# Copying the diagonal quarter of one rearrangement with ScalarE in the Gram stages

## The chip, the cores and the metric

The kernel runs on one core of one Trainium2 chip. The metric is the device time of one execution in microseconds (us). Engines are named by their work: TensorE (PE, with its weight loads PEld), VectorE (DVE), ScalarE (ACT), GpSimd (POOL) and SyncE (SP, which here only issues transfers).

## The reference, cut to what matters

Two bottleneck blocks of a ResNet follow each other on x of shape (64, 1024, 14, 14), all in float32. Each block normalises over the whole batch, so every normalisation needs statistics of all 12544 pixels (64 images of 196):

```python
def _bn(x, gamma, beta):
    mean = jnp.mean(x, axis=(0, 2, 3), keepdims=True)
    var = jnp.var(x, axis=(0, 2, 3), keepdims=True)
    xn = (x - mean) * jax.lax.rsqrt(var + EPS)
    return gamma.reshape(1, -1, 1, 1) * xn + beta.reshape(1, -1, 1, 1)

out = jax.nn.relu(_bn(_conv(x, w1, b1, 1, 0), g1, be1))      # 1x1, 1024 -> 256
out = jax.nn.relu(_bn(_conv(out, w2, b2, 1, 1), g2, be2))    # 3x3, 256 -> 256
out = _bn(_conv(out, w3, b3, 1, 0), g3, be3)                 # 1x1, 256 -> 1024
out = jax.nn.softplus(residual_scale)[0] * out
return jax.nn.relu(x + out)
```

## The kernel before

The 256 channels between the convolutions lie in `y_all`, as 128 partitions by two slots by 12544 pixels, and stay on the chip. In time the program is: the first 1x1 convolution of block 0; then for each block its 3x3 convolution (`conv2`), its Gram stage (`gram` and `conv3_stats`) and its last convolution. The last convolution of block 0 is fused with the first of block 1 (`fused`), that of block 1 stands alone (`final`).

The Gram stage is where the change is. The last normalisation needs mean and variance of 1024 channels that are a linear map of 256. The kernel doesn't compute the 1024 channels for that. It takes the 256x256 matrix of products of the 256 channels over all pixels (a Gram matrix), together with the sums of the channels, and derives the statistics from it in `conv3_stats`. TensorE sums over partitions, so for the Gram matrix the pixels have to lie on the partitions: `y_all` has to be transposed, 128 pixels of 256 channels at a time. The unit of work is a chunk of 256 pixels (`px`), 49 chunks in a stage. For each chunk eight matmul calls on a tile `zt` follow, four for each 128 pixels (half a chunk); there are six `zt` tiles (`NZT`) in rotation.

The transpose is made in one of two ways:

- `by_tensor` (line 1081): TensorE transposes into a PSUM bank, VectorE adds `c_row` and writes `zt`. Eight chunks go this way, the pieces in `still`.
- `by_vector` (line 1099): VectorE transposes blocks of 32x32 (line 1102), one instruction for each chunk. Such a transpose swaps partitions and pixels only inside groups of 32 partitions, so the data must first be moved between the four groups of 32 partitions. For this, `move(k)` (line 1058) copies piece `moved[k]` of `y_all` with transfers into a tile, its home: group j of the partitions, quarter i of the piece's pixels, to group i, column block j. There are 4x4 such pairs (i, j). Where i equals j the data keeps its partitions.

`moved` has seven pieces: `moved[0]` with 1280 pixels (five chunks) and `moved[1]` to `moved[6]` with 1536 (six chunks). For `moved[0]` and `moved[1]` all sixteen pairs are transfers. From `moved[2]` on, `move(k)` leaves out the four pairs with i equal to j and `stay(k)` (line 1051) copies them with four ScalarE activations, each on 32 partitions by 768 elements. The homes take turns, `homes[k % 3]`; in block 0 `homes[1]` is the tile `ws`, which is why the transfers of `moved[1]` and `moved[4]` have `ws` in the profile there and `home` in block 1.

Each transfer is issued on SyncE's queue or on GpSimd's. A line in `move` settles which, from the transfer's number n, and `keep_in_program_order` fixes the order of the issues. Before a piece can be moved, ScalarE applies the normalisation and relu (`normed`, two activations for a piece) and VectorE subtracts a constant for each channel (`less`, line 1041, one instruction for each slot).

The order of all this is written out by hand in the generator `pairs` (line 1109). It yields one `zt` after the other, and after certain chunks it emits the work for pieces to come. In the part with `by_tensor`, n is the number of the chunk: after chunk 3 the norms of `moved[1]`, after 4 its `less`, `move(1)` and the norms of `moved[2]`, after 5 and 6 the two halves of `less` of `moved[2]`, after 6 the norms of `moved[3]`, after 7 `move(2)` and `stay(2)`. In the part with `by_vector`, piece k emits `less` of piece k + 2 after its chunks 1 and 3, then `move(k + 2)`, the norms of `moved[k + 3]` and `stay(k + 2)`. Matmuls, activations through the helper `act`, the transposes and the issues hold the written order on their engine; what isn't held in this way is placed by the framework's planner.

Every `by_vector` chunk of a piece needs the whole piece in its home: all its transfers and, where there is one, its `stay`.

Of the kernel before, what the change touches and what calls it, by code (L numbers as in the profile page):

```python
# [88 lines left out]
def bottlenecks(ctx: ExitStack, tc: tile.TileContext, x, w1s, w2s, w3s, pars, out):  # L89
    nc = tc.nc  # L90
# [82 lines left out]
    def busy(psum, tag, n, with_=None):  # L173

        v = ident if with_ is None else with_
        for i in range(n):
            matmul(psum.tile(448, tag), v, v[:, :1].to_broadcast([P, 448]), start=True, stop=True)
# [154 lines left out]
    def act(*args, **kw):  # L332

        tc.keep_in_program_order(nc.scalar.activation(*args, **kw))  # L334

    class Conv1(Seven):
# [15 lines left out]
        def sum(self, i):  # L352
            return self.pool.tile([P, CS // 2, self.n], FP, tag=f"at{i}", name=f"at{i}")
# [195 lines left out]
    def norm_vector(s, y, aff):  # L549

        scale, shift = aff
        tc.keep_in_program_order(
            nc.vector.tensor_scalar(y, y, scale[:, s : s + 1], shift[:, s : s + 1], ALU.mult, ALU.add)
        )
        tc.keep_in_program_order(nc.vector.tensor_scalar(y, y, 0.0, None, ALU.max))
# [441 lines left out]
    def gram(psum, pool, homes, aff, minus_c, beside):  # L997
# [39 lines left out]
        def normed(a, e, slots=both):  # L1037
            for s in slots:
                norm(s, y_all[:, s, a:e], aff, act)

        def less(a, e, slots=both):
            for s in slots:
                y = y_all[:, s, a:e]
                tc.keep_in_program_order(nc.vector.tensor_scalar(y, y, minus_c[:, s : s + 1], None, ALU.add))

        def home(k):
            a, e = moved[k]
            x = homes[k % 3][:, : MS * (e - a)].rearrange("p (s j f) -> p s j f", s=MS, j=4)
            return x, a, (e - a) // 4

        def stay(k):

            x, a, run = home(k)
            for i in range(4):
                here = slice(32 * i, 32 * i + 32)
                act(x[here, :, i], y_all[here, :, a + i * run : a + i * run + run], AF.Copy)

        def move(k):
            x, a, run = home(k)
            for i, j in itertools.product(range(4), range(4)):  # L1060
                if k > 1 and i == j:
                    continue
                n = 4 * i + j if k < 2 else 3 * i + j - (j > i)
                queue = nc.gpsimd if (n % 2 if k < 2 else n in (1, 3, 6, 8, 10)) else nc.sync
                ins = queue.dma_start(
                    out=x[32 * i : 32 * i + 32, :, j], in_=y_all[32 * j : 32 * j + 32, :, a + i * run : a + i * run + run]
                )
                tc.keep_in_program_order(ins)
# [3 lines left out]
        def center_row():  # L1072

            ps = psum.tile(M, "ax")
            for s in range(MS):
                matmul(
                    ps[:, s * P : (s + 1) * P], minus_c[:, s : s + 1].to_broadcast([P, P]), ident, start=True, stop=True
                )
            act(c_row, ps, AF.Copy)

        def by_tensor(a):
            tp = psum.tile(CH * M)
            for c in range(CH):
                for s in range(MS):
                    tc.keep_in_program_order(
                        nc.tensor.transpose(
                            tp[:, (c * MS + s) * P : (c * MS + s + 1) * P],
                            y_all[:, s, a + c * P : a + (c + 1) * P], ident,
                        )
                    )  # L1090
            zt = next(zts)
            tc.keep_in_program_order(
                nc.vector.tensor_add(
                    zt[:, :, 1 : M + 1], tp.rearrange("p (c m) -> p c m", c=CH), c_row[:, None, :].to_broadcast([P, CH, M])
                )
            )
            return zt

        def by_vector(k, i):
            zt, x = next(zts), home(k)[0].rearrange("p s j f -> p (s j) f")  # L1100
            tc.keep_in_program_order(
                nc.vector.transpose(
                    zt[:, :, 1 : M + 1].rearrange("p b (n c) -> p b n c", c=32),
                    x[:, :, i * CH * 32 : (i + 1) * CH * 32].rearrange("p n (b r) -> p b n r", r=32),
                )
            )
            return zt

        def pairs():

            for a in 0, px:
                norm_vector(1, y_all[:, 1, a : a + px], aff)
                normed(a, a + px, (0,))
            normed(2 * px, 4 * px, (0,))
            center_row()
            rest = [(piece, s) for piece in still for s in range(MS)]
            (second, end), half = still[1], sum(still[1]) // 2
            for n, a in enumerate(a for piece in still for a in range(*piece, px)):
                yield by_tensor(a)
                if n == 0:  # L1120
                    busy(psum, "ax", 1)
                    norm_vector(1, y_all[:, 1, 2 * px : 4 * px], aff)
                    normed(*moved[0])
                elif n == 1:
                    less(*moved[0])
                    move(0)
                    normed(second, end, (0,))
                    normed(second, half, (1,))
                elif n == 3:
                    norm_vector(1, y_all[:, 1, half:end], aff)  # L1130
                    normed(*moved[1])
                elif n == 4:
                    less(*moved[1])
                    move(1)
                    normed(*moved[2])
                elif n == 5:
                    less(*moved[2], both[:1])
                elif n == 6:
                    less(*moved[2], both[1:])
                    normed(*moved[3])  # L1140
                elif n == 7:
                    move(2)
                    stay(2)
            for k, (a, e) in enumerate(moved):
                for i in range((e - a) // px):
                    yield by_vector(k, i)
                    if i in (1, 3) and k and k + 2 < len(moved):
                        less(*moved[k + 2], both[i // 2 : i // 2 + 1])
                        if i == 3:
                            move(k + 2)  # L1150
                            if k + 3 < len(moved):
                                normed(*moved[k + 3])
                            stay(k + 2)
                    elif i in (0, 5) and k > 1 and rest:
                        piece, s = rest.pop(0)
                        less(*piece, (s,))
            assert not rest
# [3 lines left out]
        for k, zt in enumerate(itertools.chain(pairs(), (None,))):  # L1161
            if before is not None:
                for c in range(CH):
                    first, last = k == 1 and c == 0, k == total and c == CH - 1
                    v = before[:, c]
                    for q, with_ in enumerate((v[:, : 3 * Q + 1], v[:, Q + 1 :], v[:, 2 * Q + 1 :], ends(v))):
                        here = slice(q % 2 * Q, q % 2 * Q + Q)
                        to = (upper, lower)[q // 2][here]
                        to = to[:, : 2 * Q + 1] if q == 2 else to
                        if q == 3:  # L1170
                            to = to.rearrange("p (k m) -> p k m", k=2)
                        matmul(
                            to, v[:, 1 + q * Q : 1 + q * Q + Q], with_, start=first, stop=last,
                            tile_position=(0, q % 2 * Q), skip_group_check=True,
                        )
            before = zt
            if k in beside:
                beside[k]()
# [392 lines left out]
```

## Time and profile before

| what | us |
|---|---|
| median of three runs | 1929.36 |
| lowest and highest of them | 1928.34, 1930.65 |
| the profiled execution | 1929.22 |
| its span, first to last instruction | 1927.4 |

The stretches of the span, from the windows of the trace (busy us of an engine in the stretch):

| stretch, us | TensorE | VectorE | ScalarE | GpSimd | DMA share |
|---|---|---|---|---|---|
| up to 587 (first convolution and 3x3 of block 0) | 581.8 of 586 | 487.7 | 271.0 | 68.7 | 0.71, then 0.29 |
| 587 to 651, Gram stage of block 0 | 62.2 of 64 | 53.4 | 41.3 | 24.6 | 0.78 |
| 680 to 1140, fused | 460.0 of 460 | 324.6 | 252.2 | 176.7 | 0.44 |
| 1165 to 1541, end of fused and 3x3 of block 1 | 370.3 of 376 | 336.2 | 245.1 | 73.0 | 0.63 |
| 1541 to 1609, Gram stage of block 1 | 65.6 of 68 | 53.3 | 42.5 | 25.9 | 0.75 |
| 1640 to 1927, final | 282.2 of 287 | 232.6 | 190.6 | 178.3 | 0.90 |

The DMA share is the mean busy share of the core's sixteen DMA engines. In the groups of the trace, line 334 is the helper `act`, so all held ScalarE work stands under it, and line 171 is the helper of the matmuls; such groups are told apart by the names of their tiles. Line 1065 holds the transfers of `move`, 87 issues on SyncE with a median of 596 ns and 69 on GpSimd with a median of 542 ns under the name `home`. "DMA to landing" is the time from an issue until the transfer is done.

### The profile page before, as it was taken

How to read it: one execution, taken by the hardware profiler on the slowest of the kernel's cores; microseconds unless marked ns; L12 is line 12 of the kernel's file. 1: busy time of each engine (PE TensorE's matmuls, PEld its weight loads, DVE VectorE, ACT ScalarE, POOL GpSimd, SP SyncE). 2: the span in 40 equal slices, each digit the busy share in tenths (PEclk: the TensorE clock that was granted, in tenths of full speed). 3: DMA queues.
4: the chain of work that ended last, by engine and by line, in shares of the span. 5: the costliest groups of instructions: out<-in, count | busy, mean ns of one | idle time of the engine just before them, and what ended most of it. 6: DMA issues, size and time to landing. Idle time of an engine off the chain costs nothing.

```text
span 1927.4 us, 28744 instructions
## 1 busy us (share of the span) xinstructions
PE 1905.4 (99%) x10240; PEld 1600.4 (83%) x10240; DVE 1547.5 (80%) x2491; ACT 1077.5 (56%) x2140; POOL 568.5 (29%) x684
## 2 busy tenths in 40 slices
PE   9999999999999999999999999999999999999998
PEld 5555557999997799999999999989999987555554
DVE  5778767999998867677766767689999986888886
ACT  2222214677777255555555555456777682666665
POOL 0111100211204133333434334302121041666664
PEclk9999999999999999999999999999999999999999
DMA  7777634787946534444444444258788466889998
GB/s 291 273 248 273 224 143 150 201 220 211 218 164 179 194 157 168 168 171 185 180 168 168 171 181 179 106 183 210 216 205 225 129 178 236 293 325 341 329 340 297
DMA packets 198911, 409.56 MB, mean 212 GB/s; under 512 B 37168, under 2 KB 175312, under 8 KB 182256
## 3 DMA queue, kind: packets, MB, share of 16 engines
q1 hardware_dynamic: 159808, 322.04, 48.8%
q0 software_dynamic: 33344, 34.62, 8.8%
q10 hardware_dynamic: 5616, 51.06, 6.3%
q8 instruction: 81, 1.33, 0.3%
q14 instruction: 62, 0.51, 0.1%
HBM read 263.75 MB, written 115.34 MB: 197 GB/s over the span
## 4 chain that ended last, share of the span: by engine, by line
PE 92%; DVE 4%; DMA 2%; issue 1%; ACT 1%; POOL 0%; SPq 0%; DVEq 0%; ACTq 0%; POOLq 0%
PE ay L171 17%; PE cy L171 17%; PE columns L171 13%; PE cp L171 11%; PE ap L171 10%; PE m L171 7%; PE l L171 6%; PE cx L171 5%; PE ax L171 4%; PE ps L171 1%; DMA home<-y 1%; DMA x<-mid 0%; DMA out<-x 0%; DMA x<-in_x 0%; DVE v L631 0%
## 5 line engine op out<-in xcount | busy, mean ns | idle before, releaser
L334 ACT ACTIVATE cu<-cy,scale 128x196 f32<-128x196 f32 (+1 forms) x552 | 256.3, 473 | 279.2 <-PE cy L171 273.8
L171 PE MATMUL columns<-v,ub 128*128 128x224 f32 (+1 forms) x1536 | 300.8, 337 | 0.0
L334 ACT ACTIVATE x<-x,shift 128x392 f32<-128x392 f32 x452 | 255.0, 613 | 72.6 <-POOL x L493 53.5
L171 PEld LDWEIGHTS columns<-v,ub 128*128 128x128 f32 x1536 | 269.4, 189 | 2.7
L467 DVE SCALAR_TENSOR_TENSOR x<-cp,scale,x 128x196 f32<-128x196 f32 (+1 forms) x368 | 178.0, 484 | 98.7 <-PE cp L171 96.5
L171 PE MATMUL cy<-ct,ws 128*128 128x196 f32 (+1 forms) x736 | 221.9, 383 | 1.2 <-ACT cu L334 1.2
L488 POOL TENSOR_TENSOR x<-x,cu 128x196 f32<-128x196 f32 (+1 forms) x184 | 160.1, 870 | 171.9 <-ACT cu L334 163.7
L171 PE MATMUL ay<-at,ws 128*128 128x196 f32 (+1 forms) x752 | 209.2, 381 | 0.0
L493 POOL TENSOR_TENSOR x<-x,cu 128x392 f32<-128x392 f32 x124 | 126.0, 1016 | 191.3 <-DVE x L467 191.3
L171 PEld LDWEIGHTS ay<-at,ws 128*128 128x128 f32 x752 | 136.6, 190 | 33.3
L171 PEld LDWEIGHTS cy<-ct,ws 128*128 128x128 f32 x736 | 133.6, 190 | 36.3 <-ACT cu L334 4.0
L171 PE MATMUL l<-diffs,ub 128*128 128x224 f32 (+1 forms) x768 | 149.2, 337 | 2.6 <-PE columns L171 2.6
L514 POOL TENSOR_TENSOR x<-x,cu 128x392 f32<-128x392 f32 x120 | 121.9, 1017 | 86.6 <-DVE x L467 62.2
L171 PE MATMUL m<-sums,ua 128*128 128x224 f32 (+1 forms) x752 | 145.9, 337 | 1.5 <-DVE sums L625 1.5
L334 ACT ACTIVATE au<-ay 128x196 f32<-128x196 f32 (+1 forms) x141 | 53.7, 381 | 158.0 <-PE ay L171 155.2
L171 PEld LDWEIGHTS l<-diffs,ub 128*128 128x128 f32 x768 | 134.3, 189 | 4.5 <-PE columns L171 3.9
L467 DVE SCALAR_TENSOR_TENSOR x<-cx,scale,x 128x196 f32<-128x196 f32 (+1 forms) x184 | 89.1, 484 | 56.7 <-PE cx L171 56.7
L171 PEld LDWEIGHTS m<-sums,ua 128*128 128x128 f32 x752 | 131.3, 189 | 3.2 <-DVE sums L625 2.9
L171 PE MATMUL cy<-y,w 128*128 128x196 f32 (+1 forms) x408 | 125.3, 393 | 0.0
L171 PE MATMUL cx<-y,w 128*128 128x196 f32 (+1 forms) x400 | 122.7, 392 | 0.0
L171 PE MATMUL cp<-y,ws 128*128 128x196 f32 (+1 forms) x368 | 113.7, 391 | 0.7 <-DVE x L467 0.7
L875 POOL DMA_DIRECT2D y<-f x24 | 30.8, 1521 | 275.1 <-DVE f L801 246.8
(221 smaller groups left out, 4003.3 us busy)
## 6 DMA issues: line engine op xcount, KB each, us to landing
x<-in_x SPq DMA_DIRECT2D x62, 1568.0 KB, 6.7
ub<-u SPq DMA_DIRECT2D x94, 768.0 KB, 5.6
x<-mid SPq DMA_DIRECT2D x32, 1568.0 KB, 8.1
mid<-x ACTq DMA_DIRECT2D x31, 1568.0 KB, 5.1
out<-x SPq DMA_DIRECT2D x123, 392.0 KB, 5.7
ua<-u SPq DMA_DIRECT2D x94, 256.0 KB, 3.2
u<-y POOLq DMA_DIRECT2D x48, 256.0 KB, 5.6
home<-y SPq DMA_DIRECT2D x71, 96.0 KB, 3.7
```

The costliest lines, as they stand in the source:

```text
L171: tc.keep_in_program_order(nc.tensor.matmul(*args, **kw))
L334: tc.keep_in_program_order(nc.scalar.activation(*args, **kw))
L467: nc.vector.scalar_tensor_tensor(v, bank, self.scale[:, o : o + 1], v, ALU.mult, ALU.add)
L488: nc.gpsimd.tensor_add(self.part(1, 1), self.part(1, 1), u3)
L493: nc.gpsimd.tensor_add(v, v, self.u12)
L514: nc.gpsimd.tensor_add(v, v, self.u12[:, i * self.n : (i + 1) * self.n])
L875: nc.gpsimd.dma_start(out=out_rows[3][:, o], in_=fa[:, o, :full], accum_op=ALU.add)
```

## The change

`move(1)` leaves out the four pairs with i equal to j, as `move` does from `moved[2]` on, so it issues twelve transfers in place of sixteen. Their numbers n and with them their queues are those of the later pieces: seven on SyncE and five on GpSimd in place of eight and eight. `stay(1)` is called after chunk 5 of the `by_tensor` part, between the two halves of `less` of `moved[2]`; on ScalarE its four copies stand after the norms of `moved[2]` and before those of `moved[3]`. This holds for both blocks.

```diff
         def move(k):
             x, a, run = home(k)
             for i, j in itertools.product(range(4), range(4)):
-                if k > 1 and i == j:
+                if k > 0 and i == j:
                     continue
-                n = 4 * i + j if k < 2 else 3 * i + j - (j > i)
-                queue = nc.gpsimd if (n % 2 if k < 2 else n in (1, 3, 6, 8, 10)) else nc.sync
+                n = 4 * i + j if k == 0 else 3 * i + j - (j > i)
+                queue = nc.gpsimd if (n % 2 if k == 0 else n in (1, 3, 6, 8, 10)) else nc.sync
                 ins = queue.dma_start(
...
                 elif n == 5:
                     less(*moved[2], both[:1])
+                    stay(1)
                 elif n == 6:
                     less(*moved[2], both[1:])
                     normed(*moved[3])
```

## The prediction

> **What bounds the kernel now.** I read the page's first part and the chain's shares first, to see whose time counts at all.
>
> ```profile
> PE 1905.4 (99%) x10240; PEld 1600.4 (83%) x10240; DVE 1547.5 (80%) x2491; ACT 1077.5 (56%) x2140; POOL 568.5 (29%) x684
> ...
> PE 92%; DVE 4%; DMA 2%; issue 1%; ACT 1%; POOL 0%; SPq 0%; DVEq 0%; ACTq 0%; POOLq 0%
> ```
>
> TensorE is busy 99% of the span and is 92% of the chain that ended last. So a change off TensorE earns only what it takes out of TensorE's few gaps. The edit touches the two Gram stages, 587 to 650 us (block 0) and 1544 to 1608 us (block 1). There I asked for the waits of each stage, then for TensorE's rows around them. Block 0, TensorE in order of time (start, us, what):
>
> ```profile
> 608.70 0.40 PE L171 MATMUL ap<-zt 128*64 128x129 f32 x4
> 610.39 0.55 PE L171 MATMUL cp<-zt 128*64 128x193 f32 x4 [1.29 <-DVE zt L1102]
> ```
>
> Block 1, the same view, and then the windows of that stretch (length; busy and count of PE, PEld, DVE, ACT, POOL; granted clock; DMA share; GB/s):
>
> ```profile
> 1567.16 0.55 PE L171 MATMUL cp<-zt 128*64 128x193 f32 x4 [2.20 <-DVE zt L1102]
> ...
> 1568.33 0.86 PE L171 MATMUL cp<-zt 128*64 128x193 f32 x4
> ...
> 1571.55 0.58 PE L171 MATMUL cp<-zt 128*64 128x193 f32 x4
> ...
> 1572.72 0.50 PE L171 MATMUL cp<-zt 128*64 128x193 f32 x4
> ```
>
> ```profile
> 1566.00:1568.00 2.00, 0.84 (x12) 0.78 (x14) 1.60 (x3) 0.00 (x0) 0.00 (x0) 1.00 0.93 215
> 1568.00:1570.00 2.00, 2.00 (x20) 1.72 (x18) 2.00 (x4) 0.00 (x0) 0.00 (x0) 0.57 0.03 8
> 1570.00:1572.00 2.00, 2.00 (x20) 1.79 (x18) 2.00 (x4) 1.22 (x2) 0.96 (x2) 0.58 0.06 11
> ```
>
> The reader is to see three costs: TensorE stands 1.29 us in block 0 and 2.20 us in block 1 for the first transpose of `moved[1]`, and after the longer gap the clock drops to 0.57, so that half a chunk's matmuls take 1.07 us (1568.33 to 1569.40) where 0.55 is the pace elsewhere. What the transpose waits for stands in the waits of block 1:
>
> ```profile
> DVE zt L1102 <- DMA home<-y: 5.4, 1, 5.4
> ```
>
> In block 0 this wait is 3.9 us. It ends with the last of the sixteen transfers of `move(1)`. I asked line 1065 one transfer at a time. In block 0 (home is `ws`) the seventh on SP is issued at 601.7, the eighth on GpSimd at 603.0; their answers:
>
> ```profile
> L1065 SPq DMA_DIRECT2D ws<-y x1: 749/749/749, 601.7 to 601.7; - x1
> ...
> DMA to landing us min/median/max: 5.8/5.8/5.8
> ```
>
> ```profile
> L1065 POOL DMA_DIRECT2D ws<-y x1: 539/539/539, 603.0 to 603.0; - x1
> ...
> DMA to landing us min/median/max: 6.0/6.0/6.0
> ```
>
> In block 1 the seventh on SP goes out at 1558.2 and lands 4.4 us later, the eighth on GpSimd at 1559.6 and lands 5.8 us later. Last landing before: 603.0 + 6.0 = 609.0 and 1559.6 + 5.8 = 1565.4; VectorE starts at 609.63 and 1566.40, that is 0.6 and 1.0 us after.
>
> [...] the windows 597 to 609 us have a DMA share of 0.99 to 1.07 at 217 to 233 GB/s with SP and GpSimd both issuing, so fewer transfers should land sooner. [...] (0.57 for some 3.3 us after 2.20 us idle; no drop after 1.29 us)[...] the trace has 842 ns for just this copy. [...] the copies of `stay(2)` at 826 to 846 ns beside a full DMA agree.
>
> **The change, part by part.**
>
> *Removed:* four of sixteen transfers of 96 KB in `move(1)` of each stage. SP issues seven in place of eight, GpSimd five. The two queues issue in order, so the first seven slots of SP and the first five of GpSimd keep their times (600 and 540 ns an issue, GpSimd's first and third 1339 and 1004 beside `less`) and have the same bytes ahead of them; what follows, now `move(2)` one to three slots earlier, is as large as what was there. So the traced landings of these slots are the new ones: block 0, SP 601.7 + 5.8 = 607.5, GpSimd 601.4 + 5.3 = 606.7; last 607.5, 1.5 us sooner. Block 1, SP 1558.2 + 4.4 = 1562.6, GpSimd 1558.0 + 3.9 = 1561.9; last 1562.6, 2.8 us sooner. A check by bytes: four times 98,304 bytes at 217 GB/s is 1.8 us of the engines. The traced slots are taken; the lower end, 0.4 and 0.6 us, is worked out with the second rival.
>
> *What TensorE gets.* VectorE would start at 607.5 + 0.6 = 608.1, and its tile is ready 0.76 us after (609.63 to 610.39): 608.9. TensorE ends its last chunk at 609.10. The gap is gone, with 0.2 us to spare: 1.29 us gained. Block 1: 1562.6 + 1.0 + 0.76 = 1564.4 against the end of TensorE's chunk at 1564.97: gap gone, 2.20 us gained.
>
> *The half clock* goes with its gap. From 1567.16 to 1572.72 seven half chunks take 5.56 us; at 0.548 each (604.54, 605.09, 605.63 in block 0) they take 3.84. 1.72 us. [...] I take 1.72: the profiled run has it, and its 1929.22 us lie 0.14 from the median of the runs shown, the fastest of which is only 0.9 us below.
>
> *Added:* four copies of 32x768, 4 x 0.842 = 3.4 us, on ScalarE between the norms of `moved[2]` and `moved[3]`. Beside what they run:
>
> ```profile
> 587.97 13.99 ACT L334 ACTIVATE y<-y,shift,scale 128x1280 f32<-128x1280 f32 x10
> 601.86 3.41 ACT L334 ACTIVATE home<-y 32x768 f32<-32x768 f32 x4
> 605.30 3.23 ACT L334 ACTIVATE y<-y,shift,scale 128x1536 f32<-128x1536 f32 x2
> 613.98 3.44 ACT L334 ACTIVATE home<-y 32x768 f32<-32x768 f32 x4 [5.46 <-DVE y L1044]
> ```
>
> The last two of the ten are the norms of `moved[3]`, 3.23 us, so the copies start at 598.6. They need `less` of `moved[1]`, done at 597.7 (595.80 + 1.94); no wait, and they end at 602.0, 5.5 us ahead of the last transfer. Block 1: start 1555.2, `less` done at 1554.3, end 1558.6. Behind them all moves by 3.4: norms of `moved[3]` done at 605.3, needed by `less` at 609.3 (608.1 and two transposes); `stay(2)` done at 608.7, needed at 613.5; norms of `moved[4]` done at 612.0, `stay(3)` may start at 612.4 (its `less` done). The 5.46 us of idle time takes the 3.4 up. Cost nothing; without that cover, up to 3.4 us a stage.
>
> *What is late next.* The first transpose of `moved[2]`: VectorE comes at 608.1 + 5.45 (six transposes, two `less`: 609.63 to 615.08) = 613.5. SP's queue is one slot shorter, so its last is at the former 22nd place, 606.7 + 6.0 + 0.6 = 613.3. TensorE needs the tile at 609.10 + 6 x 1.096 = 615.7, so 1.5 us are left. The first of `moved[3]`: its transfers go out after `less`, 4.3 us after VectorE's start, and were used 8.4 us later (613.95 to 622.39): 620.8, tile 621.6, wanted at 622.3: 0.7 left. Block 1 by the same sums: 1563.6 + 4.3, then 8.0 (1570.7 to 1577.7, and 1.0) gives 1575.9, tile 1576.7, wanted at 1578.1. No new gap; from there TensorE sets the end of the stage. Loads and stores behind it hang on the same tiles and move with it: in the windows after 1680 TensorE is busy 40.00 of 40 up to 1880 but for 0.16 us, though DMA has 0.91 to 0.97.
>
> *Sum:* 1.29 + 2.20 + 1.72 = 5.2 us off the profiled execution's 1929.22 (its span of 1927.4 and 1.8 around it): 1924.0; on the median of 1929.36, 1924.2.
>
> **The rivals.**
>
> *Gaps close, the clock does not count* (25%). The half clock is missing in most timed runs, or a little of block 0's spare 0.2 us is lost. [...] Against: the spread of the runs is too small to show runs without it. 3.5 us, 1925.9.
>
> *The transfers land little sooner* (13%). `move(2)` now enters GpSimd's ring three slots earlier and shares the engines with SP's last transfers. For: the DMA share is full. Against: the bytes per slot are the same. If it comes down to GpSimd's eighth alone, the landings are those of SP's eighth, 602.5 + 6.1 = 608.6 and 1558.8 + 6.0 = 1564.8: 0.4 and 0.6 us sooner, the clock as before: 1928.4.
>
> *Slower* (10%): the order of what is not held changes elsewhere. Only instructions given to `keep_in_program_order` keep their place; many of the second 3x3 stage (ScalarE's copies there, VectorE's sums and most of its steps) are placed by the planner, for which this stage's ScalarE now looks busier and SP and GpSimd emptier. The place is conv2 of block 1, 48 units from 1262 to 1541 us, where TensorE has no slack. For: from 645 to 1545 us TensorE already has 6.9 us of short waits, 2.3 of them on VectorE's `sums`. Against: the stages before and after hold their order by data, and matmuls are all held. At 0.25 us more for each unit it costs 48 x 0.25 = 12 us: 1936. It undoes the gain from 5.2 / 48 = 0.11 us a unit, and shows as slower from (5.2 + 3.9) / 48 = 0.19.
>
> **How the numbers follow.** Likeliest, gaps and half clock gone: 52%, 1924.2, own range 1923.0 to 1925.4. Range 1922.8 to 1929.5: the first three cases, without the slow one. A measurement here tells no change from one of about 0.2%, 3.9 us, so faster is under 1925.5: 48 of the first case's 52 and 3 of the second: 51%; same 39%; slower 10%.
>
> **What would show it.** Twelve issues of `move(1)`, four more ScalarE copies in each stage from 598.6 and 1555.2 without a wait; VectorE's waits at its first transpose of `moved[1]` 2.4 us in place of 3.9 and about 2.6 in place of 5.4; no TensorE gap over 0.3 us there and a clock of 1.00 in that stretch; the stage shorter by 1.3 and 3.9. Wrong if a gap of like size appears at `moved[2]` or `moved[3]`, if `less` of `moved[3]` waits for ScalarE, if conv2 of block 1 changes its length, or if the time saved is lost again where the final stage waits for loads.

## The result and the profile after

| | median us | lowest to highest | runs |
|---|---|---|---|
| before | 1929.37 | 1928.27 to 1930.65 | 9 |
| after | 1923.67 | 1923.15 to 1925.45 | 9 |

The ratio is 0.9972, 95% interval [0.9962, 0.9982]: 5.7 us less on the medians, where 5.2 was forecast. The profiled executions say the same: 1929.22 before, 1923.40 after (spans 1927.4 and 1921.6).

The first part of the page and the chain's shares, after:

```profile
PE 1903.4 (99%) x10240; PEld 1597.4 (83%) x10240; DVE 1546.8 (80%) x2491; ACT 1083.9 (56%) x2148; POOL 565.1 (29%) x678
...
PE 92%; DVE 3%; DMA 1%; issue 1%; POOL 1%; ACT 1%; SPq 0%; DVEq 0%; ACTq 0%; POOLq 0%
```

ScalarE has eight activations more (2148 for 2140), which are the four copies of each stage, and 6.4 us more of work. The chain is still TensorE's. Its shares are whole per cents, 19 us each, and too coarse for a change of 5.7 us.

To see where the 5.8 us between the two profiled executions came from, I cut both traces at events that both have: the first transpose on TensorE of each stage, and the first matmul of the convolution behind it.

| stretch | before, us | after, us | difference |
|---|---|---|---|
| up to the stage of block 0 | 587.44 | 588.22 | +0.78 |
| Gram stage of block 0 | 62.97 | 60.83 | -2.14 |
| between the two stages | 893.58 | 893.04 | -0.54 |
| Gram stage of block 1 | 64.49 | 61.34 | -3.15 |
| from there to the end | 318.92 | 318.17 | -0.75 |

5.3 of the 5.8 us lie in the two stages. The 0.5 us outside can't be told from scatter: the kernels of the experiments below have the same code there, but for one with another filler at its start, and in the profiles of the others the first stretch is 587.6 to 588.4 us long and the last 317.9 to 319.0. Now the places that the prediction had shown. TensorE in block 0, after:

```profile
608.90 0.49 PE L171 MATMUL cp<-zt 128*64 128x193 f32 x4
...
609.45 0.49 PE L171 MATMUL cp<-zt 128*64 128x193 f32 x4
```

Here there is nothing to see, and that is the reading: the second row is the first half chunk of `moved[1]`, the 27th of the stage, and it starts 0.55 us after the one before it, where before 2.02 us lay between the same two (608.37 to 610.39). In block 1 a gap is left:

```profile
1562.68 0.39 PE L171 MATMUL ap<-zt 128*64 128x130 f32 x4
1563.43 0.55 PE L171 MATMUL cp<-zt 128*64 128x193 f32 x4 [0.37 <-DVE zt L1102]
...
1564.03 0.50 PE L171 MATMUL cp<-zt 128*64 128x193 f32 x4
```

From the half chunk before it (start 1562.35) to 1563.43 are 1.08 us in place of 2.91, so 1.83 of the 2.4 us that were lost there are back and 0.5 are not. Behind it the next half chunk follows after 0.60, at the usual pace. The windows of that stretch (length; busy and count of PE, PEld, DVE, ACT, POOL; granted clock; DMA share; GB/s):

```profile
1564.00:1566.00 2.00, 2.00 (x32) 1.84 (x30) 2.00 (x3) 2.00 (x2) 0.00 (x0) 1.00 0.08 23
1566.00:1568.00 2.00, 2.00 (x34) 1.89 (x30) 2.00 (x4) 1.60 (x3) 0.69 (x2) 1.00 0.04 8
```

The clock stands at 1.00 and 32 matmuls fit into 2 us, where 20 did before. The 0.57 and 0.58 that the prediction read there are means of windows that reach over the ends of the drop. A window inside it, in the trace before, has the half:

```profile
1568.50:1571.50 3.00, 3.00 (x26) 2.56 (x24) 3.00 (x6) 0.75 (x1) 0.49 (x1) 0.50 0.00 2
```

The drop lasts from 1568.3 to 1571.7, 3.4 us. VectorE's first transposes of `moved[1]`, of both blocks:

```profile
608.20 1.30 DVE L1102 STREAM_TRANSPOSE zt<-ws 128x512 f32<-128x512 f32 x2 [1.97 <-DMA home<-y]
...
1562.66 1.31 DVE L1102 STREAM_TRANSPOSE zt<-home 128x512 f32<-128x512 f32 x2 [3.54 <-DMA home<-y]
```

The wait fell from 3.9 to 1.97 us in block 0, but only from 5.4 to 3.54 in block 1, where 2.6 was forecast. What released it is the last transfer of `move(1)`, SP's seventh. The trace on that one transfer, block 1, after:

```profile
L1065 SPq DMA_DIRECT2D home<-y x1: 1102/1102/1102, 1556.3 to 1556.3; - x1
...
DMA to landing us min/median/max: 5.7/5.7/5.7
```

This slot landed 4.4 us after its issue before the change and takes 5.7 now. Likewise GpSimd's fifth: 3.9 before, 5.2 now. The prediction had carried the old latencies over. The copies on ScalarE, block 0, after:

```profile
599.51 3.41 ACT L334 ACTIVATE ws<-y 32x768 f32<-32x768 f32 x4
602.95 3.23 ACT L334 ACTIVATE y<-y,shift,scale 128x1536 f32<-128x1536 f32 x2
606.09 3.42 ACT L334 ACTIVATE home<-y 32x768 f32<-32x768 f32 x4
609.53 3.23 ACT L334 ACTIVATE y<-y,shift,scale 128x1536 f32<-128x1536 f32 x2
612.67 3.43 ACT L334 ACTIVATE home<-y 32x768 f32<-32x768 f32 x4
```

The first row is new. No row has a bracket, so nothing waits; the 5.46 us in which ScalarE had stood still ahead of its third set of copies are used up.

### The profile page after: what moved, and what is told of

The parts are those of the page before. It is cut to its first block, busy times and chain, and to the rows that moved or that the text cites. A ratio compares the mean times of both kernels' runs of the same rounds, so it can differ in the third digit from the quotient of the medians.

```text
span 1921.6 us, 28727 instructions
## 1 busy us (share of the span) xinstructions
PE 1903.4 (99%) x10240; PEld 1597.4 (83%) x10240; DVE 1546.8 (80%) x2491; ACT 1083.9 (56%) x2148; POOL 565.1 (29%) x678
## 3 DMA queue, kind: packets, MB, share of 16 engines
q8 instruction: 81, 1.33, 0.3%
## 4 chain that ended last, share of the span: by engine, by line
PE 92%; DVE 3%; DMA 1%; issue 1%; POOL 1%; ACT 1%; SPq 0%; DVEq 0%; ACTq 0%; POOLq 0%
PE cy L171 18%; PE ay L171 17%; PE columns L171 13%; PE cp L171 11%; PE ap L171 10%; PE m L171 7%; PE l L171 6%; PE cx L171 5%; PE ax L171 5%; PE ps L171 1%; DMA home<-y 1%; POOL home L1065 1%; DMA x<-in_x 0%; DVE v L631 0%; DVE sums L625 0%
## 5 line engine op out<-in xcount | busy, mean ns | idle before, releaser
L761 ACT ACTIVATE columns<-m 128x448 f32<-128x448 f32 (+1 forms) x160 | 78.5, 490 | 59.5 <-PE m L171 57.0
```

Of the source, the lines that this page charges most:

```text
L761: nc.scalar.activation(v, m, AF.Copy)
```

## The experiments

"Interval" below is the time from the start of one half chunk on TensorE to the next; 0.548 us is the pace without a wait. Each kernel stands against the kernel before on the same chip (its median there was 1928.39 us for the first four, 1927.81 for the next four, 1929.38 for the last four).

### One block at a time

The change in block 0 alone (and the mirror image, with `b == 1`, in block 1 alone):

```diff
+                first = 0 if b == 0 else 1
-                if k > 0 and i == j:
+                if k > first and i == j:
...
                     less(*moved[2], both[:1])
-                    stay(1)
+                    if b == 0:
+                        stay(1)
```

> The change in block 0 alone. Landing theory (the gain of a stage is TensorE's gap at moved[1], closed because the last transfer lands sooner): the Gram stage of block 0 comes from 63.0 us to 60.8, that of block 1 stays at 64.5 with its 2.2 us gap and its half clock; 2.1 us faster than before. Rival, that the stages don't add because what block 0 saves is lost again in the fused stage: 0 to 1 us.

> The change in block 1 alone. Landing theory: Gram stage of block 1 from 64.5 us to 61.3, block 0 unchanged at 63.0; 3.2 us faster than before, up to 3.9 with what the final stage gave. Rival, that part of the block 1 gain came from entering the stage at another time after block 0: less than 2.5 us.

Block 0 alone: 1925.12 us, ratio 0.9984 [0.9978, 0.9991], 3.3 us less. Block 1 alone: 1926.38, 0.9989 [0.9982, 0.9996], 2.0 less. Together 5.3, against 5.7 for the whole change: the parts add up within the noise, but the larger share is block 0's, the reverse of the forecast. Neither part came as expected. Block 0's stage is only 1.5 us shorter in its profile (61.46 us), less than the 3.3 of the medians; the section on the half clock comes back to this. Block 1's 2.0 us lies under the 2.5 that its rival had named: the stage is 62.62 us long, 1.9 shorter, since new intervals of 0.74 and 1.52 us at 1591 and 1595 us took 1.2 us of the gain again. Whether they come from entering the stage at another time, as the rival has it, wasn't tried. With block 0 changed alone, block 1 on TensorE still reads as before:

```profile
1565.57 0.80 PE L171 MATMUL cp<-zt 128*64 128x193 f32 x4 [2.02 <-DVE zt L1103]
1566.59 0.86 PE L171 MATMUL cp<-zt 128*64 128x193 f32 x4
1567.66 0.86 PE L171 MATMUL cp<-zt 128*64 128x193 f32 x4
1568.73 0.71 PE L171 MATMUL cp<-zt 128*64 128x193 f32 x4
```

A wait of 2.02 us, and then starts 1.07 us apart: the half clock again. With block 1 changed alone, the wait of block 0 stands and that of block 1 shrinks to an interval of 1.49, without the half clock:

```profile
610.45 0.55 PE L171 MATMUL cp<-zt 128*64 128x193 f32 x4 [1.66 <-DVE zt L1103]
```

So each block's gap at `moved[1]` goes with its own `move(1)`.

### The half clock by itself

The kernel before, with two filler calls on TensorE, of no use to the result, in the gap of block 1:

```diff
                     yield by_vector(k, i)
+                    if b == 1 and k == 1 and i == 0:
+                        busy(psum, "ax", 2)
```

> The kernel before, but in block 1 TensorE multiplies two throw-away products of 128x448 (about 1.5 us) where it stood 2.2 us for the first transpose of moved[1]; their result is used nowhere. Nothing lands sooner. Clock theory (the half clock comes from standing idle): the gap keeps its length from chunk to chunk, 2.9 us between half chunks, but the half chunks after it run at 0.55 in place of 1.07; 1.6 us faster. Rival (the half clock has another cause, or is missing in most timed runs): 0 in the timed runs, whatever the profile shows.

1928.48 us, ratio 1.0001 [0.9993, 1.0009]: nothing gained. The profile did what was meant:

```profile
1565.12 2.10 PE L171 MATMUL ax<-ident 128*128 128x448 f32 x4
1567.61 0.55 PE L171 MATMUL cp<-zt 128*64 128x193 f32 x4 [0.39 <-DVE zt L1102]
1568.21 0.50 PE L171 MATMUL cp<-zt 128*64 128x193 f32 x4
```

The filler fills the gap, no half chunk behind it is slow, and the stage is 63.04 us long in place of 64.49, though the interval at the gap is 0.23 longer (3.14 for 2.91). So in the profiled execution the half clock costs nearly what was forecast. The mean clock of the timed runs goes the same way: 35 of the 58 runs of the kernel before on that chip have 0.999, the others 1.000; with the filler 2 of 13 have 0.999. 3.4 us at half clock take 0.0009 off the mean over 1927 us, so a run at 1.000 has no room for it.

That the median didn't follow has one cause that the runs show in part. The kernel before doesn't fall to half clock in every run: of its 106 runs in the experiments, 65 have a mean clock of 0.999 and 41 of 1.000. Their medians are 1928.95 (35 runs) and 1927.75 (23) on the first chip, 1928.95 (19) and 1927.29 (16) on the second, 1929.43 (11) and 1927.56 (2) on the third, so 1.2 to 1.9 us apart. The mean alone doesn't say where a clock was low (in some of the changed kernels 0.999 comes from the last 10 us of the program, when TensorE has no more work: with `move(2)` put later, a kernel of a section below, the granted clock is 0.92 from 1912 to 1920 us and 1.00 in the stretch of the gap), so six runs in ten is an upper bound; but for the kernel before the difference is of the size of the half clock. Counted at six runs in ten, 1.72 us are worth about 1.0 in the mean. The rest stays open: the filler's runs at 1.000 are 0.85 us slower than those of the kernel before at 1.000. A filler of fixed length also holds TensorE in runs in which the tile would have come sooner; that wasn't tried.

The same count bears on block 0 alone: its profile has the half clock in block 1, but only 6 of its 21 runs are at 0.999 (median 1926.85, the others 1925.05). So a part of its 3.3 us may be half clocks of block 1 that came less often. That wasn't tried either.

### Bytes or issues, and half of it

First, all sixteen issues kept, but the four diagonal ones with 32 of 384 pixels, and ScalarE copies the other 352:

```diff
+                m = SMALL if k == 1 and i == j else run
...
-                    out=x[32 * i : 32 * i + 32, :, j], in_=y_all[... : a + i * run + run]
+                    out=x[32 * i : 32 * i + 32, :, j, :m], in_=y_all[... : a + i * run + m]
```

> All sixteen issues of move(1) stay, in their old queues, but the four with i equal to j carry 32 of the 384 pixels (8 KB in place of 96); ScalarE copies the other 352. Bytes theory (the 16 DMA engines are full, so bytes set the landing): the engines have 0.36 MB less, the last landing is 1.2 to 1.7 us sooner in each stage, 4 to 5 us faster than before. Issue theory (what counts is the place of the last transfer in its queue, as the prediction argued): the eighth transfers go out as before and land at most 0.5 us sooner, under 1.5 us faster.

1924.91 us, ratio 0.9981 [0.9974, 0.9989], 3.5 us less. VectorE comes about as soon as in the changed kernel in block 0, and TensorE's wait is a rest of 0.23 us:

```profile
608.78 0.55 PE L172 MATMUL cp<-zt 128*64 128x193 f32 x4 [0.23 <-DVE zt L1105]
```

In block 1 the interval is 2.04 us, between 2.91 and the 1.08 of the changed kernel, without the half clock. With all sixteen issues in place the stage of block 0 is 60.84 us long, as with the change (60.83): there the gain is one of bytes on the engines, not of issues. SP's eighth transfer, issued at 602.75, lands after 4.2 us where before it took 6.1 in the same place of the queue (602.53). In block 1 a part of the gap stays. SP's eighth takes 4.9 us there where its seventh takes 3.1, and the next section has a second cause for such a step, so what is due to the issues isn't shown. The 3.5 us lie under the 4 to 5 of the theory of bytes and well over the 1.5 of the theory of issues.

Second, two of the four diagonal pairs to ScalarE:

```diff
-            for i in range(4):
+            for i in range(2 if k == 1 else 4):
...
-                if k > 1 and i == j:
+                if i == j and (k > 1 or k == 1 and i < 2):
```

> In move(1) two of the four pairs with i equal to j are left to ScalarE, fourteen transfers, seven on each queue. Landing theory: half of the effect on the landing, about 1.0 us sooner in each stage. Block 0 then has 0.3 us of its gap left, block 1 about 1.3; whether the clock still halves after 1.3 us is open (block 0 had no half clock after 1.29). 2.5 us faster if the half clock stays, 4 if it goes. Rival (only the number of issues ahead of the last counts): seven a queue is as good as seven and five, the full 5.7.

1926.07 us, ratio 0.9990 [0.9983, 0.9996], 1.7 less. Intervals of 1.16 in block 0 (from 2.02) and 1.57 in block 1 (from 2.91), no half clock. Half of the transfers took out a good half of each gap, but less of the median than expected: 2.5 us with the half clock left, 4 without it. The profiled run (1925.02) is 1.05 us under the median of its kernel, so this profile shows one of its shorter runs.

### The copies alone

The kernel before with the four ScalarE copies into a tile that nobody reads:

```diff
                     less(*moved[2], both[:1])
+                    stay_aside(1)
```

> The kernel before with all sixteen transfers, and four more ScalarE copies at the place of stay(1), into a tile that nobody reads: the added work without the removed. Theory that the copies lie in ScalarE's idle time: within 0.5 us of before. Rival, that 3.4 us more on ScalarE ahead of the norms of moved[3] hold VectorE up: 1 to 3 us slower in each stage.

1928.56 us, ratio 1.0002 [0.9994, 1.0010]. No cost shows, though the interval has room for one of up to 1.9 us, and the wait on the transfers stands as it was:

```profile
1566.07 1.30 DVE L1110 STREAM_TRANSPOSE zt<-home 128x512 f32<-128x512 f32 x2 [5.56 <-DMA home<-y]
```

### Where the landing latency of block 1 comes from

Three kernels for the 1.3 us that the last slots of `move(1)` got slower. First the changed kernel once more:

> The changed kernel as it is, once more, for the three runs beside it. 1923.7 us plus or minus 0.7; the profile is to repeat its first one: in block 1 the seventh transfer of SP lands 5.7 us after its issue and the interval of half chunks there is 1.08 us; the step in landing latency stands beside an instruction packet at about 1558.5 us.

1923.71 us, ratio 0.9972 [0.9962, 0.9982], as the first time. SP's seventh transfer lands 6.1 us after its issue, GpSimd's fifth 5.2; the interval is 1.49. So the 1.08 of the first profile is not a fixed number.

In the traces of both kernels a packet of 16 KB on the queue marked "instruction" (81 packets, 1.33 MB in the whole program) goes with the step. In the kernel before it lies at about 1561.5 us, and only transfers issued from 1558.5 on, behind the first seven of SP, land late (after 5.4 to 6.0 us, where SP's seventh took 4.4 and GpSimd's fifth 3.9). In the changed kernel it lies at about 1558.5, and the transfers in flight there land late (5.7 and 5.2 us for the same two):

```profile
q8 instruction: 1, 0.02, 17.0%
```

This is the row for that queue in the DMA view of the kernel after, 1558.5 to 1559.0 us: packets, MB, and the share of 16 engines' time, so 0.17 x 16 x 0.5 = 1.4 us of one engine, about the size of the step. In ten more profiles of this case, too, the first late transfer of block 1 was issued 1.6 to 3.2 us ahead of such a packet, which lies anywhere from 1557.9 to 1561.5 there. What these packets carry isn't shown. My estimate takes them for TensorE's own program: the page counts 20480 TensorE instructions (10240 each under PE and PEld) and 81 packets, some 253 instructions for each, so 120 more of them ahead of the stage would shift the packets by about half of their distance. To move the packet against the work in this way, the filler at the program's start was replaced by one of more and shorter instructions:

```diff
-        busy(psum, "ay", 3, ones)
+        busy(psum, "ay", 1, ones)
+        for i in range(32):
+            matmul(psum.tile(448, "ay")[:, :64], ones, ones[:, :64], start=True, stop=True)
```

> The changed kernel with the three filler matmuls at its very start replaced by one and 32 narrow ones (the filler computes nothing of the result), so that every later TensorE instruction stands about 120 places later in its stream. [...] the packets come about half a period, 4 to 5 us, earlier against the work. Theory (an instruction packet delays the transfers in flight): the step in latency moves with it; in block 1 SP's seventh lands about 4.4 us after its issue in place of 5.7, VectorE starts moved[1] at 1.3 us less of a wait (2.2 in place of 3.5) and the interval of 1.08 us there is under 0.7: 0.4 us off this stage. Rival (the packet only happens to stand there; the step comes from move(2), or from the count of transfers): latency 5.7, wait 3.5, interval 1.08 as before. Time within 1 us of the changed kernel under either, since other stages' packets move too.

The new filler took 15.4 us where the old took 4.5, so the whole is 1935.88 us (1.0036 [1.0022, 1.0050]) and tells nothing; all of the stage lies 12.0 us later, and that is taken off here. The packets came at 1565.6 and 1574.4, which is 1553.6 and 1562.4 on the clock of the changed kernel. SP's seventh and VectorE:

```profile
L1065 SPq DMA_DIRECT2D home<-y x1: 710/710/710, 1569.4 to 1569.4; - x1
...
DMA to landing us min/median/max: 4.2/4.2/4.2
```

```profile
1574.36 1.31 DVE L1102 STREAM_TRANSPOSE zt<-home 128x512 f32<-128x512 f32 x2 [2.69 <-DMA home<-y]
```

4.2 us in place of 5.7 (GpSimd's fifth 3.7 in place of 5.2), and the wait 2.69 in place of 3.54. The late ones are now the first transfers of `move(1)`: SP's first lands after 4.4 us (3.1 in the changed kernel), GpSimd's first after 4.9 (3.8). In block 0 the step moved too, to transfers that land behind the packet at 616.3. The latency step went with the packet. The tile gained less than the latency: SP's seventh was issued 1.15 us later in the stage than in the changed kernel, behind an issue that took 1.64 us in place of 0.6 (at 1565.7, beside the packet), so it landed only 0.35 us sooner. A stream thinned in this way may have helped the latency as well; against that as the whole cause stands the kernel before, where the same two transfers took 4.4 and 3.9 us with no such delay and the packet behind them. Of the 0.85 us by which the wait is shorter, 0.53 are VectorE's later start of `moved[0]`, on those first transfers. The interval came down to 0.76; and later waits of this kernel took the gain of the stage again (61.70 us long).

Then the other suspect, the prediction's second rival: `move(2)` behind VectorE's fourth transpose of `moved[0]`, so that `move(1)` has the engines alone, with the packet still where it was:

```diff
                 elif n == 6:
-                    less(*moved[2], both[1:])
                     normed(*moved[3])
-                elif n == 7:
-                    move(2)
-                    stay(2)
...
                     yield by_vector(k, i)
+                    if k == 0 and i == 3:
+                        less(*moved[2], both[1:])
+                        move(2)
+                        stay(2)
```

> The changed kernel with the second half of less(moved[2]), move(2) and stay(2) put behind VectorE's fourth transpose of moved[0], so that no transfer of move(2) is issued for 1.5 us or more after the last of move(1). Theory of the prediction's second rival (move(2) shares the engines with the last transfers of move(1)): SP's seventh in block 1 lands about 4.0 to 4.4 us after its issue in place of 5.7, VectorE waits about 2 us in place of 3.5, no gap at moved[1]. Rival (the step comes from elsewhere, an instruction packet): latency stays 5.2 us or more and the gap of 0.4 to 0.5 us stays. In either case moved[2] comes later, so the whole time is 0 to 3 us above the changed kernel.

```profile
L1065 SPq DMA_DIRECT2D home<-y x1: 847/847/847, 1556.6 to 1556.6; - x1
...
DMA to landing us min/median/max: 4.8/4.8/4.8
```

4.8 us: between the two expectations. GpSimd's fifth takes 3.9, as before the change. VectorE starts `moved[1]` at 1562.14, and TensorE has no gap at all there; the stage is 60.78 us long, in place of 61.38 in the changed kernel beside it. The whole is 1922.63 (0.9968 [0.9957, 0.9980]), 1.1 us under the changed kernel on the medians, with intervals that overlap. So on these profiles it takes both: with `move(2)` in the same engines and the packet elsewhere SP's seventh took 4.2, with the packet there and `move(2)` later 4.8, with both 5.7 to 6.1. Neither can be called the whole cause, and in block 0 there is more: in the second profile of the changed kernel SP's latency there goes from 4.8 to 5.8 us between its fifth and sixth transfer, with no such packet between 599 and 608 us.

### Further in the same direction

The diagonal of `move(0)` to ScalarE as well; or six and six of the twelve issues of `move(1)` to the two queues; and both at once, with six and six for `move(0)` too.

```diff
-                if k > 0 and i == j:
+                if i == j:
...
                     less(*moved[2], both[:1])
+                    stay(0)
                     stay(1)
```

```diff
-                queue = nc.gpsimd if (n % 2 if k == 0 else n in (1, 3, 6, 8, 10)) else nc.sync
+                queue = nc.gpsimd if (n % 2 if k < 2 else n in (1, 3, 6, 8, 10)) else nc.sync
```

> The change taken one step further: move(0) leaves out the diagonal too, stay(0) stands ahead of stay(1). Landing theory: 0.33 MB less ahead of everything, the waits left in the changed kernel (0.2 to 0.4 us at moved[0] in block 0, 0.4 to 0.6 at moved[1] in block 1) go: 0.5 to 1.2 us faster than the changed kernel, 6.2 to 6.9 faster than before. Rival, that ScalarE is now full (6.6 us of work for a piece of 6.6 us of matmuls, and no idle time left to take 2.9 us more up): the norms of moved[3] come late for VectorE, slower than the changed kernel by 1 to 3 us.

> The changed kernel with the twelve transfers of move(1) taking turns, six on each queue, in place of seven on SyncE and five on GpSimd. Landing theory: in block 1 the seventh on SyncE was the last to land (1562.0 against 1561.3 on GpSimd), so the last landing comes 0.3 to 0.7 us sooner there and the rest of the gap closes: 0.3 to 0.7 us faster than the changed kernel. Rival, that GpSimd's sixth, held up by VectorE, is now the last: no gain or 0.5 us slower.

> The two versions that gave the most put together: ScalarE also copies the diagonal quarter of move(0), and move(0) and move(1) each give six transfers to SP and six to GpSimd. If the rest of the gaps is queue time, the stages come to about 60.4 and 60.9 us and the whole to 1921.5 us; if they gained by the same wait, the whole is that of the better of the two, 1922.4; if one of them was chance, 1923.

| | median us | ratio to before | stage of block 0 | stage of block 1 |
|---|---|---|---|---|
| the change | 1923.71 | 0.9972 [0.9962, 0.9982] | 61.04 | 61.38 |
| diagonal of `move(0)` too | 1922.36 | 0.9969 [0.9956, 0.9981] | 60.40 | 61.45 |
| six and six | 1922.98 | 0.9972 [0.9961, 0.9984] | 60.40 | 60.94 |
| both | 1922.97 | 0.9968 [0.9956, 0.9981] | 60.40 | 60.65 |

The first of the three removes TensorE's wait at `moved[1]` altogether in block 1 as well; VectorE's rows, blocks 0 and 1:

```profile
606.45 1.30 DVE L1102 STREAM_TRANSPOSE zt<-ws 128x512 f32<-128x512 f32 x2 [1.25 <-DMA ws<-y]
...
1561.42 1.30 DVE L1102 STREAM_TRANSPOSE zt<-home 128x512 f32<-128x512 f32 x2 [2.34 <-DMA home<-y]
```

In block 0 all three come to 60.40 us, with no odd interval left. In block 1 an interval of 0.8 to 1.5 near 1591 us remains, as in the first profile of the change (0.89); VectorE has four instructions of `combine_w3` ahead of a transpose there (2.5 us, lines 151 to 154). None of the three can be told from the change by these runs. (The second and third row were run on another chip than the first and last, each against the kernel before beside it.)

## Why the prediction was right, and where it was not

**What bounds the kernel.** Right. What the stages lost in length is what TensorE's gaps lost, and 5.3 of 5.8 us came out of the two stages that the edit touches.

**The transfers removed.** Right in kind, mis-sized in one term. The landings were taken from the traced slots. Counted from the start of its stage, SP's seventh landed at 19.7 us in block 0, where 607.5 - 587.44 = 20.1 was forecast, and the wait became 1.97 us (2.4 forecast). In block 1 that slot took 5.7 us in place of the 4.4 carried over; it landed at 19.9 us, where 1562.6 - 1543.99 = 18.6 was forecast. So the last landing came 1.9 and 1.5 us sooner, for 1.5 and 2.8: the prediction's own check by bytes, 1.8 us, was nearer to both than the slots that it took instead. "The same bytes ahead of them" was true and not enough: the second rival had named the sharing with `move(2)`, and the prediction gave it 13% as a whole and nothing as a part. The moved packet and the delayed `move(2)` point to two causes, of which the prediction knew one.

**The gaps.** Block 0: 1.29 us forecast, 2.14 came. The bracket of a row holds only the idle time just ahead of it; the interval of 2.02 us is 1.47 over the pace. Two later intervals of 0.71 us, at 625.2 and 639.7, went as well (2 x 0.16), and that at `moved[0]` shrank from 1.17 to 0.92. These are 2.04 of the 2.14. Some of it is scatter: with block 0 as before the stage is 62.44 to 62.97 us long in three profiles (before, block 1 alone, filler), with it changed 60.83 to 61.46 in three, and the interval at `moved[0]` is 0.55 to 1.17 and 0.80 to 1.56. Block 1: 2.20 forecast; the interval fell by 1.83, since the latency left 0.5 us standing. TensorE's idle time of 0.37 us there is over the 0.3 that the prediction had named as a sign.

**The half clock.** Right in the profiles: the granted clock was 0.50 behind the gap before and is 1.00 there after, and with the filler in the gap it is 1.00 without the change. As a term for the median it was too large, 1.72 where at most about 1.0 is its mean worth. That the profiled run lay 0.14 us from the median was read as a sign that every run has it, and the median would lie there too with six runs in ten. In the profiled pair it is 1.63 (three and a bit intervals of 1.07 to 1.08): 1.83 + 1.63, less 0.33 of a new wait at 1592.5, are 3.13 of the 3.15 us of that stage. What sets it off was not shown: 2.20 us of idle time had it behind them (2.02 and 2.38 in two other kernels), 1.29 to 1.66 us had not; and 41 of the 106 runs of the kernel before have a mean clock of 1.000, so no such drop, with idle times that no trace shows. A single trace can't price it.

**The copies.** Right, at nothing: no wait at their start, the idle 5.46 us gone, and the copies alone leave the time where it was (+0.02% [-0.06, +0.10]).

**What is late next.** Right in the main: neither `moved[2]` nor `moved[3]` opened a gap in either block. The 0.33 us at 1592.5 lie beyond the pieces that were worked out; the second profile of the change doesn't have them.

**The sum.** 5.2 forecast, 5.7 measured: block 0 gave 0.85 more than its term, block 1's gap 0.4 and its clock 0.1 less, its new wait 0.3, and 0.5 us came from outside the stages, which no term had. The sum was nearer than its terms, since errors of both signs met in it; that is luck. On the medians, with at most 1.0 us for the clock, some 0.6 of the 5.7 us have no term, and the interval (3.5 to 7.3 us) covers that.

**The rivals.** The first (3.5 us, 1925.9) is 2.2 us off. Its premise holds in part: four runs in ten of the kernel before, or more, have no half clock by their mean clock (41 of 106 at 1.000), and the gaps alone gave 3.5 us in the profiled pair (2.04 + 1.83 - 0.33). The second holds as a part of block 1's latency, and not for its time (1928.4). The slower one falls: TensorE and VectorE run the same instructions in the same order in both kernels, the other queues differ by the edit alone, and from 1165 to 1541 us TensorE's busy time is 370.7 us against 370.3 before, and the stretch between the two stages is 893.04 us long against 893.58.

## What to carry to other kernels

Where one engine sets the time, price a change off it by that engine's gaps, and count the whole chain of intervals behind a gap, not its bracket alone: a lead that the second engine regains can also take away its later short waits (here 2 x 0.16 us in block 0). A landing latency read from one trace need not hold with something else in flight: SP's seventh, 96 KB in the same slot, took 4.4 us before and 5.7 after. If a change moves transfers into another's time, give it a span of a microsecond, and not the traced value, and set a check by bytes beside it. And look at the spread of the clock over many runs (here 65 of 106 at 0.999, the others at 1.000) before an effect of one profile goes into a sum for the median.

## What the runs showed of the hardware

- One 16 KB packet of the queue marked "instruction" goes with a step of about 1.3 to 1.5 us in the landing of 96 KB transfers that are in flight: 5.7 us with it, 4.2 with the packet moved away, though it has a sixth of one transfer's bytes. The packets were moved in one kernel only, in which an issue of SP came late as well, and what makes the delay wasn't tried.
- In the profiles of three kernels (before, block 0 alone, copies alone) TensorE stood idle for 2.20, 2.02 and 2.38 us, and the granted clock was then 0.50 to 0.51 over 3.4 us. Idle times of 1.29 to 1.66 us (block 0 in four profiles, block 1 with the small transfers) had no such drop behind them. By the mean clock (0.999 in 65 of 106 runs), it happens to the kernel before in at most about six of ten runs.
- One set of transfers slowed the landing of another. While SP and GpSimd both issue, from 597 to 609 us of the kernel before, the DMA share is 0.99 to 1.07 at 217 to 233 GB/s; and holding one set of twelve, seven on SP and five on GpSimd, back by 2 to 3 us took 0.9 to 1.3 us off the landing latency of SP's last transfer of the set ahead of it (4.8 us, from 5.7 and 6.1).
